# A stacked attention kernel: L1's weight preparation placed among the first batch's top-k, and the last batch's gathered sums shared between GpSimd and DVE

## The chip, the cores and the metric

The kernel runs on one core of a Trainium2 chip. The metric is the device time of one execution in microseconds (us); smaller is better. The core has a matrix engine (TensorE, "PE" in the profile, its weight loads "PEld"), a vector engine (VectorE, "DVE"), an activation engine (ScalarE, "ACT"), GpSimd ("POOL"), and SyncE ("SP"), whose queue issues the DMA transfers. Each engine executes its own instructions strictly in order; between engines there are semaphores.

## The reference, cut to what matters

Four layers are applied to x (32 batches, 128 channels, 1024 positions) with a context ctx of the same shape.

```python
x = L0(x, ctx, ctx, ctx, mask, ...)   # attention within chunks of 64 positions, 8 heads, then layer norm
x = L1(x, ctx, Wq, Aq, Bq, ...)       # 32 query heads, 8 key/value heads; every weight is W + 2 * A @ B (A, B of rank 16)
x = L2(x, ctx, ctx, ctx, mask, ...)   # as L0 with other weights
x = L3(ctx, x, ...)                   # points: see below

def L3(x_loc, x, ...):                # the first 3 channels of ctx are 3-D points
    idx = top_k(-squared_distances(x_loc), 30)          # for each of 1024 points, per batch
    rel = pts[idx] - pts                                 # gathered coordinates
    sph = (rho, theta, phi)(rel)
    h   = three small batch-normalised layers over ALL batches (sph)
    att = softmax(h over the 30 neighbours)
    return x + sum_k x[idx_k] * att_k
```

(The top-k runs over all 128 context channels, as the reference writes it: the distance is the product of whole ctx columns.) The batch norm in L3 needs all batches' gathered coordinates before anything after it can start. So the kernel has two halves: the loop over 32 batches (L0, L1, L2, the top-k and the gathering of coordinates), and after it the batch norms and the weighted sums.

## The kernel before, in words

**The loop over batches.** For batch b, `layers(b)` is a generator that emits L0, L1 and L2 in small pieces, mostly matmuls on PE, row maxima and normalisation on DVE (`mx`, `rc`, `on`) and exponentials on ACT (`s`). Beside it runs `neighbours(b)`, a generator of 64 steps: eight tiles of 128 points, for each four rounds of "find the 8 largest" on DVE. A step is either `V.max` (profile: MAX8) or `V.max_index` with `V.match_replace` (FIND_INDEX8, MATCH_REPLACE8). The same steps emit the distances of the next tile (`distances`: PE matmuls `pd`, an ACT copy to `v`), the norms of the next batch's points (`norms`: `sq`, `xx_ps`, `xp`, `xe`), the gather of the batch before (`gather`) and the angles of a finished pair of batches (`sph`).

**What sets the order.** `InOrder` keeps the instructions of DVE, ACT, PE and GpSimd in the order in which the Python code emits them. The main loop hands out the steps: each piece of `layers(b)` yields a weight, the weights of a batch sum to 65.3 (`STEPS`), and after each piece so many steps of `neighbours(b)` are emitted that their number keeps up with the sum (`done * STEPS < at * LN`). DMA issues on SP are not held in this order; a scheduler places them, and SP executes them in order.

**L1's weights.** Before the loop, at lines 452 to 465, the products 2·A·B are added to the four weights. They are cut into 10 slices of 128 partitions x 8 x 256 (4 for q, 1 for k, 1 for v, 4 for o). For each slice: one load of 1 MB into `w` (pool `wst`, 3 buffers), 8 matmuls of 16 x 128 by 16 x 256 into `lora_ps` (pool `mm_ps`, 2 buffers), 8 DVE instructions that add the product to `w`, and one store of 1 MB to DRAM (`w1_d`). Every batch loads the slices from there again (`w1_slice`). Only when all this is emitted come `norms(0)` and `distances(0, 0, h)` and then the loop.

**The gather.** `gather()` walks over n = 0 to 511: batch, tile of 128 points, half of the 30 neighbours. For one n: a DMA broadcasts rows of indices into `oh` (`spread`, 3 buffers, issued two n ahead), DVE compares them with the partition number to make one-hot matrices (`compare`, one n ahead), PE multiplies them with a table in three groups of 5 (`gps`, one buffer), ACT copies each group into `sel` (2 buffers), and GpSimd sums `sel` in six instructions: two adds of 128x360, one multiply by the mask `el`, adds of 128x180 and 128x90, and one of 128x45 into `co`. The gather of batch b is emitted in the steps of batch b + 1. The 16 n of the last batch are therefore emitted after the last `layers`, in `neighbours(B, coordinates)` and the loop behind it (lines 942 to 945), where the angles of batches 28 and 29 (`sph(14)`) are emitted between them; then comes `sph(15)` for the last two batches, and then the batch norms.

Of the kernel before, what the change touches and what calls it, by code (L numbers as in the profile page):

```python
# [10 lines left out]
F32 = mybir.dt.float32  # L11
# [4 lines left out]
ALU = mybir.AluOpType  # L16
# [4 lines left out]
P = 128  # L21
B, C, T = 32, 128, 1024
# [9 lines left out]
KV = NKV * HD  # L32
R = 16
# [23 lines left out]
def bcast(ap, axis, n):  # L57

    v = ap.unsqueeze(axis)
    shape = list(v.shape)  # L60
    shape[axis] = n
    return v.to_broadcast(shape)
# [3 lines left out]
def stacked_xattn_kernel(ctx: ExitStack, tc: tile.TileContext, io: dict, out: bass.AP):  # L66
    nc = tc.nc
    V, S, PE, G = nc.vector, nc.scalar, nc.tensor, nc.gpsimd
# [42 lines left out]
    NKB, SW = T // P, 256  # L111
# [12 lines left out]
    act = sa.enter_context(tc.tile_pool(name="act", bufs=7))  # L124
# [129 lines left out]
    lofs, cos, els, ohs = {}, {}, {}, {}  # L254
    H = KN // 2

    def spread(n):

        oh = kw.tile([P, H, P], BF16, name="oh", bufs=3)
        b, t, h = n // (2 * NT), n // 2 % NT, n % 2  # L260
        nc.sync.dma_start(
            oh.rearrange("p k n -> p (k n)"),
            hi_d[b * NT + t, h * H : (h + 1) * H, :].rearrange("k n -> (k n)").partition_broadcast(P),
        )
        ohs[n] = oh

    def compare(n):


        b, t, h = n // (2 * NT), n // 2 % NT, n % 2  # L270
        V.tensor_scalar(ohs[n], ohs[n], iota_p, None, ALU.is_equal)
        if h == 0:
            els[b, t] = kw.tile([P, NT, KN], BF16, name="el")
            V.tensor_tensor(els[b, t], iota_l, bcast(lofs[b][:, t, 0:KN], 1, NT), ALU.is_equal)

    def gather():

        last = 2 * NT * B
        for n in range(last):
            b, t, h = n // (2 * NT), n // 2 % NT, n % 2  # L280
            if n == 0:
                spread(0)
                spread(1)
                yield
                compare(0)
                yield
            if b % 2 == 0 and t == 0 and h == 0:
                cos[b // 2] = kw.tile([P, 3, CW], F32, name="co")
            co = cos[b // 2]
            oh = ohs.pop(n)  # L290
            sel = kw.tile([P, H, 9, NT], F32, name="sel")
            for k0 in range(0, H, 5):
                gps = g_ps.tile([P, 5, 9 * NT], F32, name="gps", tag="g")
                for k in range(5):
                    PE.matmul(
                        gps[:, k, :],
                        oh[:, k0 + k, :],
                        ctab[:, b].rearrange("p i e l -> p (i e l)"),
                        start=True,
                        stop=True,  # L300
                    )
                S.copy(sel[:, k0 : k0 + 5].rearrange("p k i l -> p k (i l)"), gps)
                if k0 == 0 and n + 2 < last:
                    spread(n + 2)
                if k0 == H // 3 and n + 1 < last:
                    compare(n + 1)
                if k0 == 2 * H // 3:

                    a = sel.rearrange("p k (i e) l -> p (k i) e l", e=3)
                    a0 = a[:, :, 0, :]  # L310
                    G.tensor_tensor(a0, a0, a[:, :, 1, :], ALU.add)
                    G.tensor_tensor(a0, a0, a[:, :, 2, :], ALU.add)
                    a3 = a0.rearrange("p (k i) l -> p k i l", i=3)
                    ks = slice(h * H, (h + 1) * H)
                    G.tensor_tensor(a3, a3, bcast(els[b, t][:, :, ks].rearrange("p l k -> p k l"), 2, 3), ALU.mult)
                    G.tensor_tensor(a0[:, :, 0:4], a0[:, :, 0:4], a0[:, :, 4:8], ALU.add)
                    G.tensor_tensor(a0[:, :, 0:2], a0[:, :, 0:2], a0[:, :, 2:4], ALU.add)
                    c0 = ((b % 2) * NT + t) * KN + h * H
                    G.tensor_tensor(
                        co[:, :, c0 : c0 + H].rearrange("p i k -> p k i"), a3[:, :, :, 0], a3[:, :, :, 1], ALU.add  # L320
                    )
                yield
# [126 lines left out]

    for nm, n in (("q", T), ("k", KV), ("v", KV), ("o", T)):
        at = act.tile([R, T], F32, name=f"at_{nm}", tag="a4")
        nc.sync.dma_start(at, io[f"A{nm}T"])
        bt = act.tile([R, n], F32, name=f"bt_{nm}", tag="a4")
        nc.sync.dma_start(bt, io[f"B{nm}"])
        for j in range(n // SW):
            c0 = j * SW
            w = wst.tile([P, NKB, SW], F32, name="w1")
            nc.sync.dma_start(w, io[f"W{nm}"].rearrange("(k p) n -> p k n", p=P)[:, :, c0 : c0 + SW])  # L460
            for kb in range(NKB):
                ps = mm_ps.tile([P, SW], F32, name="lora_ps", tag="mm")
                PE.matmul(ps, at[:, kb * P : kb * P + P], bt[:, c0 : c0 + SW], start=True, stop=True)
                V.scalar_tensor_tensor(w[:, kb, :], ps, LORA, w[:, kb, :], ALU.mult, ALU.add)
            nc.sync.dma_start(w1_d[nm][j], w.rearrange("p k n -> p (k n)"))

    def w1_slice(nm, j):
        w = wst.tile([P, NKB, SW], F32, name="w1")
        nc.sync.dma_start(w.rearrange("p k n -> p (k n)"), w1_d[nm][j])
        return w  # L470
# [447 lines left out]
    V, S, PE, G = (InOrder(tc, e) for e in (nc.vector, nc.scalar, nc.tensor, nc.gpsimd))  # L918
    for _ in norms(0):
        pass  # L920
    for h in range(2):
        distances(0, 0, h)
    coordinates = gather()
    LN = NT * TK
    STEPS = 65.3
    for b in range(B):
        near = neighbours(b, coordinates)
        done, at = 0, 0.0
        for w in layers(b):
            if w > 0.0:  # L930
                for a in tails:
                    next(a, None)
            at += abs(w)
            while done < LN and done * STEPS < at * LN:
                next(near, None)
                done += 1
        assert abs(at - STEPS) < 1e-6, at
        for _ in near:
            pass
# [9 lines left out]
    V, S, PE, G = nc.vector, nc.scalar, nc.tensor, nc.gpsimd  # L949
# [9 lines left out]
    with ExitStack() as st:  # L959
# [37 lines left out]
        def bn_coefs(name, mu, var, n, g, bb):  # L997

            a = l3.tile([P, n], F32, name=f"a_{name}")
            cst = l3.tile([P, n], F32, name=f"c_{name}")  # L1000
            S.activation(a, var, AF.Sqrt, bias=eps_t)
            V.reciprocal(a, a)
            V.tensor_tensor(a, a, g, ALU.mult)
            V.tensor_tensor(cst, mu, a, ALU.mult)
            V.tensor_tensor(cst, bb, cst, ALU.subtract)
            return a, cst
# [46 lines left out]
        for c in range(NCK):  # L1053
            x = [co[:, c, i, :] for i in range(3)]
            y = []
            for j in range(6):
                z = work(f"z{j}")
                if j < NZ:
                    ps = z_ps.tile([P, CW], F32, name="z_ps")
# [8 lines left out]
            for i in range(3):  # L1068
                if i < NH:
                    ps = h_ps.tile([P, CW], F32, name="h_ps")  # L1070
# [14 lines left out]
        for c in range(NCK):  # L1085
# [4 lines left out]
            ps = h_ps.tile([P, CW], F32, name="h_ps")  # L1090
# [4 lines left out]
        a3, c3 = bn_coefs("3", *moments("3", st3, 1), 1, g3, b3)  # L1095
# [55 lines left out]
    steps, done = deque(), []  # L1151
# [36 lines left out]
    def load(b):  # L1188

        x3t = ab.tile([P, NT, C], F32, name="x3t", bufs=3)  # L1190
        nc.sync.dma_start(x3t, x3_d[:, b * NT * C : (b + 1) * NT * C])
        at = ab.tile([P, NT * KR], F32, name="att")
        nc.sync.dma_start(at, att_d[:, b * NT * KR : (b + 1) * NT * KR])
        h1 = ab.tile([P, 2 * NT * NG], BF16, name="h1")
        nc.sync.dma_start(h1, hl_d[:, b].rearrange("p e n -> p (e n)"))
        hl = ab.tile([P, 2, NT, NG, 2], BF16, name="hl")
        S.copy(hl.rearrange("p e t g c -> p (e t g) c"), bcast(h1, 2, 2))
        att = ab.tile([P, NT * KR], F32, name="attt")
        V.transpose(att, at)
        ap = ab.tile([P, 2, NT, NG, 2], F16, name="ap")  # L1200
        a0, a1 = (ap[:, i].rearrange("p t g c -> p (t g) c") for i in range(2))
        S.activation(a0, bcast(att, 2, 2), AF.Copy, scale=AS)
        V.scalar_tensor_tensor(a1, bcast(att, 2, 2), AS, a0, ALU.mult, ALU.subtract)
        xs = ab.tile([P, 2, NT, C], F16, name="xs", bufs=3)
        S.activation(xs[:, 0], x3t, AF.Copy, scale=XS)
        V.scalar_tensor_tensor(xs[:, 1], x3t, XS, xs[:, 0], ALU.mult, ALU.subtract)
        return x3t, xs, hl, ap
# [21 lines left out]
    for b in range(B):  # L1229
        x3t, xs, hl, ap = ready  # L1230
        for T4 in range(NT // 4):
# [3 lines left out]
            for t4 in range(4):  # L1235
                t = 4 * T4 + t4
# [13 lines left out]
                for h in range(2):  # L1250

                    ps = at_ps.tile([P, NG // 2, 4, 2, NT], F32, name="at_ps")
# [71 lines left out]
```

## Time and profile before

| | us |
|---|---|
| three runs, median (lowest to highest) | 7793.85 (7787.23 to 7795.2) |
| the profiled execution, its own time | 7792.81 |
| its span from first to last instruction | 7791.0 |
| PE, DVE, ACT, POOL busy in it | 6478.1, 6707.4, 4266.8, 2870.5 |
| granted TensorE clock, mean | 0.895 |

The page cuts the span into 40 slices of 195 us and prints one digit for each: the share of a slice in which an engine was busy, in tenths. The timeline prints one line per instruction, or per run of equal ones: start, duration, engine, source line, operation, output<-inputs, the count, and in brackets how long the engine had been idle and what ended that. Everything inside the main loop has line L54, because it goes through the helper of `InOrder`; it is told apart by the tiles' names. The profiled execution is 1.04 us faster than the median of the runs shown.

### The profile page before, as it was taken

The numbers are of one execution on the slowest core, as the hardware profiler recorded it, in microseconds if no ns is written. First come the engines' busy times: TensorE is split into PE (matmuls) and PEld (weight loads), VectorE is DVE, ScalarE is ACT, GpSimd is POOL, SyncE is SP. The second block draws the span as 40 slices with busy tenths as digits, with TensorE's granted clock in tenths as the row PEclk, the third lists the DMA queues.
The fourth block names the chain that finished last, engine by engine and source line by source line (L and its number), as shares of the span: only waits on it lengthen the run. The fifth ranks groups of instructions, "written<-read, shape, count | busy, mean of one in ns | idle before, by whom it ended". The sixth has DMA issues, their size and how long they took to land.

```text
span 7791.0 us, 152295 instructions
## 1 busy us (share of the span) xinstructions
PE 6478.1 (83%) x60911; PEld 4501.3 (58%) x61331; DVE 6707.4 (86%) x9607; ACT 4266.8 (55%) x10867; POOL 2870.5 (37%) x3788
## 2 busy tenths in 40 slices
PE   6888888888888888888888888888888882958998
PEld 3666565656565666566666666666656561435555
DVE  4888888888888888888989888888888886989998
ACT  1555555555555555555555555555555552357787
POOL 0144444444444434444444444444444446000000
PEclk9999898989898989898888888888889895979999
DMA  5333332333333323333333333333333223013332
GB/s 148 103 127 125 103 114 98 117 102 114 102 114 107 115 91 115 107 115 108 114 105 114 110 114 107 112 107 114 110 105 110 98 101 113 0 55 97 97 93 74
DMA packets 327717, 813.28 MB, mean 104 GB/s; under 512 B 95712, under 2 KB 184320, under 8 KB 284768
## 3 DMA queue, kind: packets, MB, share of 16 engines
q1 hardware_dynamic: 327008, 803.53, 31.3%
q8 instruction: 482, 7.90, 0.4%
q14 instruction: 227, 1.86, 0.1%
HBM read 703.54 MB, written 66.32 MB: 99 GB/s over the span
## 4 chain that ended last, share of the span: by engine, by line
PE 46%; DVE 30%; ACT 14%; POOL 4%; issue 3%; DMA 2%; SPq 0%; another core or an unknown queue 0%; DVEq 0%; ACTq 0%; POOLq 0%
PE tr L54 9%; PE s_ps L54 7%; PE o_ps L54 7%; DVE idx L54 5%; PE q_ps L54 5%; DVE top L54 5%; PE pd L54 4%; DVE v L54 4%; ACT s L54 4%; POOL sel L54 3%; PE gps L54 2%; DVE oh L1241 2%; PE h_ps L1042 2%; PE k_ps L54 2%; DVE mx L54 2%
## 5 line engine op out<-in xcount | busy, mean ns | idle before, releaser
L54 POOL TENSOR_TENSOR sel<-sel 128x360 f32<-128x360 f32 (+2 forms) x2048 | 1550.8, 757 | 2867.5 <-ACT sel L54 2747.1
L54 DVE MAX8 top<-v 128x8 f32<-128x1024 f32 x1024 | 1248.5, 1219 | 91.4 <-ACT v L54 81.4
L54 ACT ACTIVATE s<-s_ps,mx 128x64 f32<-128x64 f32 (+1 forms) x5120 | 1194.0, 349 | 118.0 <-DVE mx L54 117.6
L54 DVE FIND_INDEX8 idx<-top,v 128x8 uint32<-128x1024 f32 x1024 | 1246.9, 1218 | 0.0
L54 ACT COPY sel<-gps 128x360 f32<-128x360 f32 x1536 | 714.2, 465 | 946.4 <-PE gps L54 892.4
L54 ACT COPY pt<-tr 128x512 f32<-128x512 f32 x768 | 450.8, 587 | 895.9 <-PE tr L54 894.6
L54 DVE MATCH_REPLACE8 v<-top,v 128x1024 f32<-128x1024 f32 x768 | 928.5, 1209 | 0.0
L54 PEld LDWEIGHTS <-oh 128*128 128x128 bf16 x7680 | 483.6, 107 | 501.7 <-issue 429.8
L54 PE MATMUL gps<-ctab,oh 128*128 128x72 bf16 x7680 | 549.9, 208 | 265.7 <-ACT sel L54 262.4
L54 DVE TENSOR_REDUCE mx<-s_ps 128x8 f32<-128x512 f32 (+1 forms) x768 | 524.0, 682 | 283.6 <-PE s_ps L54 283.4
L54 PE MATMUL tr<-ident,s 128*128 128x128 f32 x3072 | 575.2, 310 | 183.8 <-ACT s L54 177.3
L1162 PE MATMUL po<-wt,xs 128*128 128x512 f16 x2048 | 692.5, 383 | 0.0
L54 PEld LDWEIGHTS tr<-ident,s 128*128 128x128 f32 x3072 | 447.1, 158 | 422.9 <-ACT s L54 237.5
L1258 PE MATMUL at_ps<-wz,oh 128*128 128x64 f16 x8192 | 572.3, 194 | 137.8 <-ACT wt L1263 65.8
L1258 PEld LDWEIGHTS <-oh 128*128 128x128 f16 x8192 | 442.3, 99 | 396.6 <-issue 181.0
L54 PE MATMUL pd<-cx 128*128 128x512 f32 x1024 | 640.7, 711 | 0.8 <-ACT v L54 0.8
L54 POOL TENSOR_TENSOR sel<-sel,el 128x360 f32<-128x360 f32 x512 | 615.3, 1202 | 40.2
L54 PE MATMUL tr<-half 128*128 128x512 bf16 x1536 | 522.7, 426 | 113.3 <-ACT ot L54 68.3
L1263 ACT CAST wt<-at_ps 128x512 f16<-128x512 f32 x1024 | 544.0, 595 | 121.3 <-PE at_ps L1258 120.6
L1241 DVE TENSOR_TENSOR oh<-iot,hl 128x8192 f16<-128x8192 bf16 x128 | 565.6, 4419 | 4.3 <-PE at_ps L1258 2.7
L54 ACT ACTIVATE v<-pd,nxx 128x512 f32<-128x512 f32 x512 | 358.8, 701 | 319.6 <-PE gps L54 133.8
L54 PE MATMUL q_ps<-xt,w 128*128 128x128 f32 x4096 | 507.4, 279 | 1.7
(232 smaller groups left out, 11851.4 us busy)
## 6 DMA issues: line engine op xcount, KB each, us to landing
oh<-hi_d SPq DMA_DIRECT2D x512, 480.0 KB
w<-w_q SPq DMA_DIRECT2D x128, 1024.0 KB
w<-w_o SPq DMA_DIRECT2D x128, 1024.0 KB
w<-w_k SPq DMA_DIRECT2D x32, 1024.0 KB
w<-w_v SPq DMA_DIRECT2D x32, 1024.0 KB
wz<-wp SPq DMA_DIRECT2D x256, 128.0 KB
cx<-in_ctx SPq DMA_DIRECT2D x32, 512.0 KB
xin<-in_x SPq DMA_DIRECT2D x32, 512.0 KB
```

The source lines that it names most:

```text
L54: return lambda *a, **k: self.tc.keep_in_program_order(f(*a, **k))
L1042: PE.matmul(ps, d[:, i, :], x[i], start=(i == 0), stop=(i == len(x) - 1))
L1162: PE.matmul(po[0], xs[:, i, l, :], wt[:, j, l, :, :].rearrange("p t n -> p (t n)"), start=(n == 0), stop=(n == 4 * NT - 1),)
L1241: V.tensor_tensor(pairs(oh2), pairs(bcast(iot, 1, 2 * NG)), by_twos(h2, P // 2), ALU.is_equal)
L1258: PE.matmul(ps[:, g], oh[:, gg], wz_now[:, :, t4 * NG + gg], start=True, stop=True)
L1263: S.copy(wt[:, i, :, t4, :].rearrange("p l (q g) -> p l q g", g=NG)[:, :, :, h * (NG // 2) : (h + 1) * (NG // 2)], ps[:, :, :, i, :].rearr ...
```

## The change

Two places are edited.

1. The preparation of L1's weights becomes a generator `prepared()` that yields after each of the 10 slices, with the loads of two slices issued ahead. It is emitted in the main loop at b = 0, before `layers(0)`; after each slice, 5 steps of `neighbours(0)` are emitted. So 50 of the 64 top-k steps of batch 0 stand between the slices and 14 are left for `layers(0)`; `norms(0)` and the first distances now come before the preparation. Its PE and DVE instructions go through `InOrder` now, so their line becomes L54.
2. For the last batch, the six summing instructions of odd n are issued on DVE instead of GpSimd. They stand in DVE's order where they stood in the code: behind `compare(n + 1)` and, in `neighbours(B)`, behind a step of the angles.

```diff
                 if k0 == 2 * H // 3:
+                    E = V if b == B - 1 and n % 2 else G
                     a = sel.rearrange("p k (i e) l -> p (k i) e l", e=3)
                     a0 = a[:, :, 0, :]
-                    G.tensor_tensor(a0, a0, a[:, :, 1, :], ALU.add)
-                    G.tensor_tensor(a0, a0, a[:, :, 2, :], ALU.add)
+                    E.tensor_tensor(a0, a0, a[:, :, 1, :], ALU.add)
+                    E.tensor_tensor(a0, a0, a[:, :, 2, :], ALU.add)
...

-    for nm, n in (("q", T), ("k", KV), ("v", KV), ("o", T)):
-        at = act.tile([R, T], F32, name=f"at_{nm}", tag="a4")
-        nc.sync.dma_start(at, io[f"A{nm}T"])
-        bt = act.tile([R, n], F32, name=f"bt_{nm}", tag="a4")
-        nc.sync.dma_start(bt, io[f"B{nm}"])
-        for j in range(n // SW):
-            c0 = j * SW
+    def prepared():
+        def load(nm, j):
             w = wst.tile([P, NKB, SW], F32, name="w1")
-            nc.sync.dma_start(w, io[f"W{nm}"].rearrange("(k p) n -> p k n", p=P)[:, :, c0 : c0 + SW])
+            nc.sync.dma_start(w, io[f"W{nm}"].rearrange("(k p) n -> p k n", p=P)[:, :, j * SW : j * SW + SW])
+            return w
+
+        slices = [(nm, n, j) for nm, n in (("q", T), ("k", KV), ("v", KV), ("o", T)) for j in range(n // SW)]
+        ws = [load(nm, j) for nm, n, j in slices[:2]]
+        for i, (nm, n, j) in enumerate(slices):
+            if j == 0:
+                at = act.tile([R, T], F32, name=f"at_{nm}", tag="a4")
+                nc.sync.dma_start(at, io[f"A{nm}T"])
+                bt = act.tile([R, n], F32, name=f"bt_{nm}", tag="a4")
+                nc.sync.dma_start(bt, io[f"B{nm}"])
+            w = ws.pop(0)
             for kb in range(NKB):
                 ps = mm_ps.tile([P, SW], F32, name="lora_ps", tag="mm")
-                PE.matmul(ps, at[:, kb * P : kb * P + P], bt[:, c0 : c0 + SW], start=True, stop=True)
+                PE.matmul(ps, at[:, kb * P : kb * P + P], bt[:, j * SW : j * SW + SW], start=True, stop=True)
                 V.scalar_tensor_tensor(w[:, kb, :], ps, LORA, w[:, kb, :], ALU.mult, ALU.add)
             nc.sync.dma_start(w1_d[nm][j], w.rearrange("p k n -> p (k n)"))
+            if i + 2 < len(slices):
+                ws.append(load(slices[i + 2][0], slices[i + 2][2]))
+            yield
...
         near = neighbours(b, coordinates)
         done, at = 0, 0.0
+        if b == 0:
+            for _ in prepared():
+                for _ in range(5):
+                    next(near, None)
+                    done += 1
         for w in layers(b):
```

More of the change, by code (lines that the diff above doesn't have):

```diff
@@ L307, in gather @@
                 if k0 == 2 * H // 3:
+                    E = V if b == B - 1 and n % 2 else G
                     a = sel.rearrange("p k (i e) l -> p (k i) e l", e=3)
                     a0 = a[:, :, 0, :]
-                    G.tensor_tensor(a0, a0, a[:, :, 1, :], ALU.add)
-                    G.tensor_tensor(a0, a0, a[:, :, 2, :], ALU.add)
+                    E.tensor_tensor(a0, a0, a[:, :, 1, :], ALU.add)
+                    E.tensor_tensor(a0, a0, a[:, :, 2, :], ALU.add)
                     a3 = a0.rearrange("p (k i) l -> p k i l", i=3)
                     ks = slice(h * H, (h + 1) * H)
-                    G.tensor_tensor(a3, a3, bcast(els[b, t][:, :, ks].rearrange("p l k -> p k l"), 2, 3), ALU.mult)
-                    G.tensor_tensor(a0[:, :, 0:4], a0[:, :, 0:4], a0[:, :, 4:8], ALU.add)
-                    G.tensor_tensor(a0[:, :, 0:2], a0[:, :, 0:2], a0[:, :, 2:4], ALU.add)
+                    E.tensor_tensor(a3, a3, bcast(els[b, t][:, :, ks].rearrange("p l k -> p k l"), 2, 3), ALU.mult)
+                    E.tensor_tensor(a0[:, :, 0:4], a0[:, :, 0:4], a0[:, :, 4:8], ALU.add)
+                    E.tensor_tensor(a0[:, :, 0:2], a0[:, :, 0:2], a0[:, :, 2:4], ALU.add)
                     c0 = ((b % 2) * NT + t) * KN + h * H
-                    G.tensor_tensor(
+                    E.tensor_tensor(
                         co[:, :, c0 : c0 + H].rearrange("p i k -> p k i"), a3[:, :, :, 0], a3[:, :, :, 1], ALU.add
```

## The prediction

> **What bounds the kernel now.** I read the 40 slices first, to see which stages the edit touches and which engine is full there.
>
> ```profile
> PE   6888888888888888888888888888888882958998
> DVE  4888888888888888888989888888888886989998
> POOL 0144444444444434444444444444444446000000
> ```
>
> Only the two ends of the loop matter: slice 1, where DVE is at 4, and slices 33 and 34, where PE falls to 2. (In the middle PE and DVE are both at 8, and nothing is edited.) Next the timeline of DVE from 68 to 152 us shows how the preparation ends and batch 0 begins:
>
> ```profile
> 68.92 0.76 DVE L464 SCALAR_TENSOR_TENSOR w<-lora_ps,w 128x256 f32<-128x256 f32 x2 [8.09 <-DMA w<-in_Wq]
> 70.65 0.42 DVE L464 SCALAR_TENSOR_TENSOR w<-lora_ps,w 128x256 f32<-128x256 f32 x1 [0.98 <-PE lora_ps L463]
> 71.50 0.42 DVE L464 SCALAR_TENSOR_TENSOR w<-lora_ps,w 128x256 f32<-128x256 f32 x1 [0.43 <-PE lora_ps L463]
> ...
> 144.04 1.23 DVE L54 MAX8 top<-v 128x8 f32<-128x1024 f32 x1 [12.01 <-ACT v L54]
> 145.31 0.09 DVE L54 MATCH_VALUE_LOAD idx<-top,v 128x8 f32 x1
> 145.38 1.22 DVE L54 FIND_INDEX8 idx<-top,v 128x8 uint32<-128x1024 f32 x1
> 146.64 0.09 DVE L54 MATCH_VALUE_LOAD v<-top,v 128x8 f32 x1
> 146.72 1.21 DVE L54 MATCH_REPLACE8 v<-top,v 128x1024 f32<-128x1024 f32 x1
> 147.96 1.23 DVE L54 MAX8 top<-v 128x8 f32<-128x1024 f32 x1
> ...
> 151.76 0.68 DVE L54 TENSOR_REDUCE mx<-s_ps 128x8 f32<-128x512 f32 x1
> ```
>
> In the preparation one DVE addition takes 0.42 us and then waits 0.43 to 0.46 us for the next product: 0.87 us each. So DVE has gaps, but gaps of 0.4 us, in which no top-k instruction of 1.2 us fits. Top-k starts at 144.04, the first row maximum of L0 at 151.76.
>
> Third, busy time by stretch, for the preparation, batch 0 from its first row maximum to the start of batch 1 (306 us), and the last batch's sums:
>
> ```profile
> core 0: us, PE busy (x) PEld busy (x) DVE busy (x) ACT busy (x) POOL busy (x), PEclk, DMA share, GB/s
> 37.00:132.00 95.00, 71.47 (x163) 40.85 (x162) 33.60 (x80) 2.34 (x2) 0.00 (x0) 1.00 0.67 234
> 152.00:306.00 154.00, 137.11 (x1222) 99.27 (x1232) 131.96 (x208) 77.19 (x232) 8.16 (x13) 0.94 0.22 74
> 6459.00:6546.00 87.00, 20.16 (x220) 14.97 (x219) 35.81 (x43) 22.92 (x48) 79.59 (x101) 0.50 0.24 77
> ```
>
> Batch 0 has two full engines: PE 137 of 154 us, DVE 132. The last sums have one: POOL, 80 of 87. Their timeline shows the cycle of one n:
>
> ```profile
> 6512.00 2.45 POOL L54 TENSOR_TENSOR sel<-sel 128x360 f32<-128x360 f32 x2
> 6512.08 0.46 ACT L54 COPY sel<-gps 128x360 f32<-128x360 f32 x1 [2.42 <-POOL co L54]
> 6513.08 0.46 ACT L54 COPY sel<-gps 128x360 f32<-128x360 f32 x1 [0.55 <-PE gps L54]
> 6514.09 0.46 ACT L54 COPY sel<-gps 128x360 f32<-128x360 f32 x1 [0.54 <-PE gps L54]
> 6514.52 1.11 POOL L54 TENSOR_TENSOR sel<-sel,el 128x360 f32<-128x360 f32 x1
> ```
>
> ACT starts filling a `sel` when POOL has finished the n two before; the three copies take 2.5 us, hidden behind POOL's sum of the n between.
>
> **Part 1, the preparation.** Removed: the stretch before 144 us in which nothing but slices runs. Added in front of L0: 50 top-k steps. Both are serial on DVE, so I walk along DVE.
>
> Start. On SP batch 0's `cx` load moves ahead of all slices, to where `at_q` is issued now (31.94 us). Landing: between 2.3 us (bt_q, 64 KB, issued 34.44, used 36.71) and 5.7 us (this load at 104.03, landed at 109.73, among stores); I take 5, near the 5.3 us of the first 1 MB slice, so 37. Then table load 1.28 and square 1.06 on ACT, `xx_ps` 3.57 on PE, and from there to the end of the second `pd` 7.79 (135.07 to 142.86): 50.7. PE's first `lora_ps` is behind that; its product reaches DVE about 1.3 us later (a buffer freed at 42.64, the addition that uses it at 43.95), at 52.0. Eight additions, 7 x 0.87 + 0.42, end at 58.5. The other 9 slices have two products waiting, as after the stall at 68.92: first addition to the end of the eighth (75.39) is 6.5 us, 58.5 in all. DMA is not late: a slice is needed every 15 us and its load and store take about 5 each; the later `at`/`bt` loads and the stores wait on SP behind one another, but all have a block of top-k ahead of their use.
>
> Steps. Two steps take 3.92 us (144.04 to 147.96); a tile's last round lacks the replacement, 2.6. A tile is 3 x 3.92 + 2.6 = 14.4; 50 steps are six tiles and two steps, 90.1 us. `pd` (PE) and `v` (ACT) run beside them, as do `norms(1)` on ACT, PE and POOL, and are not late: a tile's last `v` is due three steps (5 us) after its `pd` is emitted.
>
> So the first row maximum comes at 58.5 + 58.5 + 90.1 = 207.1 instead of 151.8: **+55.3 us**. The matmuls of L0's start are ready by then.
>
> Given back in batch 0. DVE loses about 88 us of top-k there, but PE does not: of the 15 `pd` sets in 152 to 306 us (16.9 us of PE) 11 move out, 12.4 us, and `xx_ps`, 3.4 us. PE's idle time is 16.9 us; the waits of PE show 5.0 as one gap (`tr` for the layer norm's output, late because top-k stands between its DVE instructions), and the rest as 0.7 us waits for ACT copies that stay. I take 5 of the gap and 2 more: 12.4 + 3.4 + 7 = **22.8 us**. Bounds: 15.8 (no idle time returns) to 32.7 (all of it does). PE is late next.
>
> The Trainium skill ("Perfetto Trace Analysis", Identifying the Most-Contended Engine) speaks against my reading: matmul busy time is a bad measure, weight-load busy time a better one. By its measure batch 0 has 55 us of slack on PE, and the sum below would be about -17; that is my second rival.
>
> **Part 2, the sums.** Eight of the last 16 sums leave POOL. The trace has no such sum on DVE. Its 480-element add takes 0.65 us undisturbed (6554.46) and its six-element one 0.17, so 360, 180, 90 and 45 elements are near 0.53, 0.35, 0.26 and 0.21: 3 x 0.53 + 0.82 + starts = 2.7 us. Beside POOL it is slower: from 6491.6 to 6497.4 DVE needed 5.8 us for instructions that take 3.46 alone (four of 0.66, two of 0.41), and POOL 5.86 for a sum of 4.6. So 2.7 (alone) to 4.5 (x 1.67) on DVE, 4.6 to 5.9 on POOL; I take about 3.6 and 5.2, since half of DVE's sum falls into POOL's wait.
>
> That wait is new. POOL's next even n needs the `sel` of the even n just finished: the 2.5 us of copies are no longer hidden. A pair is 2.5 + 5.2 + 0.1 = 7.8 us against 9.6 now (nine sums from 6502.4 to 6545.8: 4.82 each).
> While `sph(14)` runs (n = 497 to 503), DVE is the late one: two compares and `el` 1.9, an angle step near 6.3 (octants, 5.4 to 7.9 beside POOL), then the odd sum behind it, with compare(n + 1) and so PE and ACT waiting behind that. Such a pair is 11 to 12 us against 10.8 (seven sums in 37.8 us). One is only arctangents on ACT: shorter. Walking it: sums 497, 499, 501, 503 end at 6467, 6476, 6488, 6499.5; POOL starts 504 at 6499.3 (today 6507.1, with 503 done before it at 6502.4), then every 7.8 us: 510 ends at 6527.8, DVE's 511 at 6529. The subtraction `r` of `sph(15)`, today at 6545.86, starts 17 us earlier: **-17 us**. Behind it nothing changes. Bounds: -22 (DVE's sum wholly hidden, POOL 4.6: pairs of 7.2) to 0 (sums on the two engines never overlap: 4.6 + 2.7 + 2.5 = 9.8 a pair).
>
> The lower bound is what the Trainium skill ("SBUF — State Buffer", SBUF: two separate sides) says: a DVE instruction with two SBUF inputs and a GpSimd one lock the shared port for a whole instruction each. The row above disagrees: 3.46 + 4.6 us of work in 5.86. By the rule the sum would be +32.
>
> **Sum.** 55.3 - 22.8 - 17 = +15.5 us on the profiled execution's 7792.81; it lies 1 us under the median, so I put the change on 7793.85: **7809 us**, 0.2% slower. That is about what a measurement of this kernel can tell from no change (0.2%, 15.6 us), so the sign of the sum is firmer than the verdict.
>
> **Rivals.**
> 1. Batch 0 gives back all of PE's idle time, 32.7 us, or the slices run at the clock to which `q_ps` warms between 143.08 and 150.72 us (1.91 to 1.02 us for two matmuls; some 1.5 us a slice). +5.6 or about 0: 7794 to 7800, no change. For it: many small waits vanish with the top-k. Against: `lora_ps` stayed slow through 21 us of unbroken work.
> 2. Faster: PE is not really full in batch 0, its ends being modelled. With weight loads busy 99 of 154 us, up to 55 us come back: 55.3 - 55 - 17 = -17, 7777. It turns negative when batch 0 returns 38 us and reads as faster at 54. Against: the 1222 matmuls leave gaps of under 0.7 us, and the batches with a gather on top take longer.
> 3. The tail gains nothing (no overlap, or DVE's angles delay the odd sums more): +32, 7826. For it: the slowed rows above; in the first half DVE has more to do than POOL.
> That the top-k hides nothing at all is half of the forecast: DVE pays for both in turn.
>
> **Chances and range.** Forecast 0.51 (its range, +2 to +30, straddles the limit: 0.27 slower, 0.24 same), rival 1 0.15 (0.13 same, 0.01 each side), rival 2 0.12 (faster), rival 3 0.22 (slower). So slower 0.50, same 0.37, faster 0.13. The range leaves out most of rival 2 and the worst of rival 3: 7782 to 7829.
>
> **What would show it.** First row maximum of L0 near 207 us; additions in runs of eight over 6.5 us between top-k blocks of 9 us; batch 0 from there to batch 1's start about 131 us with PE over 90% busy; at the end POOL idle 2.5 us before each even sum, odd sums of 2.7 to 4.5 us on DVE, and from the end of batch 31 to `r` 17 us less than now. Wrong would make it: batch 0 in under 116 us, slices much under 6.5 us, or sums that do not overlap.

## The result, and the profile after

Over 19 runs of each kernel the change takes 7814.5 us (median; 7794.44 to 7829.16), the kernel before 7789.79 (7775.65 to 7795.2): a ratio of 1.0032, with a 95% interval of 1.0025 to 1.0039. It is slower, by about 25 us (20 to 30 by the interval); 15.5 were forecast, and 7814.5 lies in the range given.

The profiled execution took 7808.19 us, 15.4 more than that of before. That this is nearly the forecast is chance, as the sum by stages shows. From the timelines I read the starts of a few landmarks: DVE's first top-k instruction, the first row maximum of L0, ACT's first `q` of batch 1, the transpose of batch 31's indices that ends its top-k, and the subtraction `r` of `sph(15)`. The stretches between them, in us:

| | first top-k | first row maximum | batch 1 starts | batch 0 | loop to batch 31's indices | from there to `r` | `r` to the end |
|---|---|---|---|---|---|---|---|
| before | 144.0 | 151.8 | 306.0 | 154.2 | 6121.6 | 118.3 | 1245.1 |
| after | 56.2 | 201.6 | 337.3 | 135.7 | 6113.4 | 109.3 | 1246.4 |
| after minus before | | +49.8 | +31.3 | -18.5 | -8.2 | -9.0 | +1.3 |

The edit stands in the start, batch 0 and the stretch to `r`: 49.8 - 18.5 - 9.0 = **+22.3 us**, against +24.7 between the medians. One profile does not fix batch 0 that well: in three experiments below that leave the start as it was, batch 1 starts at 308.6 to 312.1 us and not at 306.0; by them the sum would be +16 to +20. The loop in between is not edited; it took 6121.6 and 6113.4 us in these two executions (mean granted clock 0.895 and 0.896) and 6012.8 to 6106.8 in those of the experiments below (0.899 to 0.911), with the same code. Whole times therefore move by more than most of the effects looked for here: a ratio stands only between runs measured together, and the stretches of the edited stages are the finer reading.

The 40 slices after, for the three engines shown before:

```profile
PE   5888888888888888888888888888888882958998
DVE  6588888888888888888988888888888898989998
POOL 0044444444444444444444444444444445000000
```

DVE rose from 4 to 6 in slice 1, and fell to 5 in slice 2, which holds batch 0 without its top-k: the top-k has been moved, not hidden. At the end, in slice 34, POOL goes from 6 to 5 and DVE from 6 to 8. DVE's timeline at the first block:

```profile
55.82 0.42 DVE L54 SCALAR_TENSOR_TENSOR w<-lora_ps,w 128x256 f32<-128x256 f32 x1 [0.43 <-PE lora_ps L54]
56.16 1.22 DVE L54 MAX8 top<-v 128x8 f32<-128x1024 f32 x1
...
63.98 1.23 DVE L54 MAX8 top<-v 128x8 f32<-128x1024 f32 x1
65.13 0.74 DVE L54 SCALAR_TENSOR_TENSOR w<-lora_ps,w 128x256 f32<-128x256 f32 x2
66.84 0.42 DVE L54 SCALAR_TENSOR_TENSOR w<-lora_ps,w 128x256 f32<-128x256 f32 x1 [0.98 <-PE lora_ps L54]
67.69 0.42 DVE L54 SCALAR_TENSOR_TENSOR w<-lora_ps,w 128x256 f32<-128x256 f32 x1 [0.43 <-PE lora_ps L54]
...
71.16 0.42 DVE L54 SCALAR_TENSOR_TENSOR w<-lora_ps,w 128x256 f32<-128x256 f32 x1 [0.43 <-PE lora_ps L54]
71.50 0.08 DVE L54 MATCH_VALUE_LOAD idx<-top,v 128x8 f32 x1
```

Each block of five steps runs 9 us without a gap; behind it two products wait ("x2"), and from the third on PE is late again by 0.43 to 0.98 us for every addition. A slice costs 6.4 us (65.13 to 71.50), though two of its products were made under the top-k.

Busy time in two stretches, batch 0 (first row maximum to batch 1) and batch 31's indices to `r`; of the kernel before:

```profile
152.00:306.00 154.00, 137.11 (x1222) 99.27 (x1232) 131.96 (x208) 77.19 (x232) 8.16 (x13) 0.94 0.22 74
6427.50:6545.80 118.30, 29.61 (x286) 20.85 (x285) 51.33 (x69) 29.83 (x61) 98.40 (x123) 0.51 0.25 79
```

And of the kernel after (columns: length, then PE, PEld, DVE, ACT and POOL busy with their instructions, PE's clock, DMA share, GB/s):

```profile
201.60:337.30 135.70, 121.01 (x1181) 89.02 (x1182) 55.83 (x106) 68.18 (x217) 5.26 (x7) 0.97 0.25 84
6450.70:6560.00 109.30, 29.74 (x286) 20.62 (x285) 80.34 (x117) 29.83 (x61) 64.71 (x76) 0.51 0.28 86
```

In batch 0 DVE lost 76 us of work. The batch is 18.3 us shorter, of which 16.1 is time that PE is no longer busy (the `pd` and `xx_ps` that moved out are 16.0 of it); PE's idle time only falls from 16.9 to 14.7. In the last sums POOL has 34 us less to do and DVE 29 more, for 9 us.

### The profile page after: what moved, and what is told of

Read it like the earlier page. It is cut to its first block, busy times and chain, and to the rows that moved or that the text cites. A ratio compares the mean times of both kernels' runs of the same rounds, so it can differ in the third digit from the quotient of the medians.

```text
span 7806.4 us, 152322 instructions
## 1 busy us (share of the span) xinstructions
PE 6494.1 (83%) x60918; PEld 4502.2 (58%) x61331; DVE 6740.3 (86%) x9655; ACT 4267.1 (55%) x10867; POOL 2835.7 (36%) x3740
## 3 DMA queue, kind: packets, MB, share of 16 engines
q1 hardware_dynamic: 327008, 803.53, 31.3%
## 4 chain that ended last, share of the span: by engine, by line
PE 46%; DVE 31%; ACT 14%; issue 3%; POOL 3%; DMA 2%; SPq 0%; another core or an unknown queue 0%; ACTq 0%; DVEq 0%; POOLq 0%
PE tr L54 9%; PE s_ps L54 7%; PE o_ps L54 7%; DVE idx L54 6%; DVE top L54 5%; PE q_ps L54 5%; DVE v L54 4%; PE pd L54 4%; ACT s L54 4%; PE gps L54 2%; DVE oh L1259 2%; PE h_ps L1060 2%; PE k_ps L54 2%; POOL sel L54 2%; DVE oh L54 2%
## 5 line engine op out<-in xcount | busy, mean ns | idle before, releaser
L54 POOL TENSOR_TENSOR sel<-sel 128x360 f32<-128x360 f32 x2016 | 1525.9, 757 | 2878.2 <-ACT sel L54 2759.6
L54 DVE MAX8 top<-v 128x8 f32<-128x1024 f32 x1024 | 1248.0, 1219 | 67.8 <-ACT v L54 57.5
L54 ACT ACTIVATE s<-s_ps,mx 128x64 f32<-128x64 f32 (+1 forms) x5120 | 1194.1, 349 | 116.3 <-DVE mx L54 116.0
L54 DVE FIND_INDEX8 idx<-top,v 128x8 uint32<-128x1024 f32 x1024 | 1246.4, 1217 | 0.0
L54 ACT COPY sel<-gps 128x360 f32<-128x360 f32 x1536 | 714.1, 465 | 940.8 <-PE gps L54 907.2
L54 ACT COPY pt<-tr 128x512 f32<-128x512 f32 x768 | 450.8, 587 | 896.5 <-PE tr L54 890.7
L54 DVE MATCH_REPLACE8 v<-top,v 128x1024 f32<-128x1024 f32 x768 | 928.4, 1209 | 0.0
L54 DVE TENSOR_REDUCE mx<-s_ps 128x8 f32<-128x512 f32 (+1 forms) x768 | 522.9, 682 | 311.6 <-PE s_ps L54 306.7
L54 PEld LDWEIGHTS <-oh 128*128 128x128 bf16 x7680 | 483.8, 107 | 495.8 <-issue 402.1
L54 PE MATMUL gps<-ctab,oh 128*128 128x72 bf16 x7680 | 550.4, 208 | 259.9 <-ACT sel L54 236.3
L54 PE MATMUL tr<-ident,s 128*128 128x128 f32 x3072 | 575.6, 310 | 184.1 <-ACT s L54 177.3
L54 PEld LDWEIGHTS tr<-ident,s 128*128 128x128 f32 x3072 | 447.2, 158 | 422.5 <-ACT s L54 237.5
L1276 PE MATMUL at_ps<-wz,oh 128*128 128x64 f16 x8192 | 573.8, 194 | 137.9 <-ACT wt L1281 66.4
L54 PE MATMUL pd<-cx 128*128 128x512 f32 x1024 | 655.9, 726 | 1.7 <-ACT v L54 1.7
L54 POOL TENSOR_TENSOR sel<-sel,el 128x360 f32<-128x360 f32 x504 | 608.7, 1208 | 39.5
L54 PE MATMUL tr<-half 128*128 128x512 bf16 x1536 | 522.0, 425 | 110.5 <-ACT ot L54 66.5
L54 ACT ACTIVATE v<-pd,nxx 128x512 f32<-128x512 f32 x512 | 358.7, 701 | 428.1 <-remote 146.1
L54 PE MATMUL q_ps<-xt,w 128*128 128x128 f32 x4096 | 505.1, 278 | 1.6
```

The lines of the kernel that those rows point to most:

```text
L54: return lambda *a, **k: self.tc.keep_in_program_order(f(*a, **k))
L1276: PE.matmul(ps[:, g], oh[:, gg], wz_now[:, :, t4 * NG + gg], start=True, stop=True)
```

## Experiments

**Each part alone.** The first kernel has the new preparation and all sums on GpSimd, the second the old preparation and the sums by turns.

```diff
 # part 1 alone
-                    E = V if b == B - 1 and n % 2 else G
+                    E = G
```

> Part 1 alone: the preparation among the top-k, all sums on GpSimd. Theory (the two parts add up; the loss is all in part 1): first row maximum of L0 at 201.6 us and batch 1 at 337 as in the changed kernel, so +31 us there, and the stretch from the last batch's index transpose to r at 118 us as before; the whole +31 us, 0.4%. Rival (the parts are not independent, or the main loop in between pays for some of it): less than +25 or more than +37 with these two stretches unchanged.

> Part 2 alone: the last batch's odd sums on DVE, the preparation as before. Theory: the start is as before (row maximum at 151.8, batch 1 at 306), the stretch from the last index transpose to r falls from 118.3 to 109.3 us, the whole -9 us. My prediction had -17; rival (the changed kernel's tail was disturbed by what came before it): 101 us for the stretch.

Part 1 alone: first row maximum at 201.7, batch 1 at 335.8 (306.0 before: +29.8), 117.9 us to `r`. The time is 7792.8 us, a ratio of 1.0039 (1.0026 to 1.0053): 0.39% of the 7763.72 us that the kernel before took beside it is 30 us (20 to 41), the same as the stage shows. Part 2 alone: a start as before (151.9) and 109.2 us to `r`, 9 less; a ratio of 0.9995 (0.9986 to 1.0004), in which 9 us (0.12%) still fits. In its profile batch 0 took 160.2 us instead of 154.2 with no edit there; two more kernels below that leave the start as it was have 155.8 and 157.5. PE's idle time in the four is 16.6 to 18.1 us; the rest is PE's busy time, 137.1 to 142.1 us at granted clocks of 0.91 to 0.95. So about 6 us of this stretch are not settled by one profile. In the other stretches each part does alone what it does in the changed kernel, and the loss is part 1's.

**How much top-k between the slices.** Part 1 alone with 2 steps and with none after each slice:

```diff
-                for _ in range(5):
+                for _ in range(2):      # and range(0)
```

> Part 1 without the top-k steps: loads two slices ahead and the norms first, but 0 steps between the slices; all 64 steps stay in batch 0. Theory (the loss is the 50 steps, 1.76 us each, that DVE pays in turn with the slices): slices of 7.0 us from 49.8 us on, end near 120, row maximum near 128 instead of 151.8, batch 0 as long as before (154 us), the whole -24 us. Rival (the loss is in the slices, their loads or the new place of the norms): row maximum at 152 or later, no gain or a loss.

> Part 1 with 2 steps between the slices instead of 5, so 20 steps moved. Theory: 20 x 1.76 = 35 us more of preparation than with none, less 5 us because two products wait at each slice; row maximum near 153; batch 0 gives back about 0.38 us a step, 7 us; the whole about -5 us, between the kernels with 0 and with 5 steps and on the line through them. Rival (a few steps are hidden in the gaps of the preparation and only the later ones cost): as fast as with 0 steps, -24 us.

| steps after a slice | first row maximum | batch 0 | batch 1 starts | whole time, ratio |
|---|---|---|---|---|
| (before) | 151.8 | 154.2 | 306.0 | |
| 0 | 137.9 | 157.9 | 295.8 | 0.9990 (0.9981 to 0.9999) |
| 2 | 154.6 | 149.9 | 304.5 | 0.9993 (0.9984 to 1.0002) |
| 5 | 201.7 | 134.1 | 335.8 | 1.0039 (1.0026 to 1.0053) |

Part 1 holds a gain, the loads issued ahead, and a loss, the top-k; the last 30 steps cost 31.3 us at batch 1, 1.04 us a step. The first 20 cost only 8.7, 0.43 a step. At the first row maximum, which does not carry the unsettled us of batch 0, it is 16.7 us for the first 20 and 47.1 for the last 30: 0.84 and 1.57 a step. The first steps are cheaper because without steps the slices have a wait that the steps then cover. DVE's first row maximum without steps came 10 us later than I had expected (128), the whole gained about 8 us and not 24, and the timelines of that run say why. PE's:

```profile
90.42 0.63 PE L54 MATMUL lora_ps<-bt_v,at_v 16*128 16x256 f32 x1
101.25 3.35 PE L54 MATMUL lora_ps<-bt_o,at_o 16*128 16x256 f32 x7 [10.21 <-DMA bt_o<-in_Bo]
```

And that of SP's queue:

```profile
91.53 0.32 SPq L474 DMA_DIRECT2D w_v<-w  x1
91.91 0.43 SPq L458 DMA_DIRECT2D w<-in_Wo  x1
92.43 1.10 SPq L466 DMA_DIRECT2D at_o<-in_AoT  x1
93.58 0.82 SPq L468 DMA_DIRECT2D bt_o<-in_Bo  x1
```

The two factors of `o`, 64 KB each, are issued on SP only behind the store of the slice before (which waits for its last addition) and behind a load of 1 MB. They are asked for at 92.4 us, when PE already needs them, and are there at 101.2. With 2 steps after a slice PE has no such wait, and in the changed kernel DVE never waits for a load; a block of top-k covers this.

**Does batch 0's top-k hold PE up?** The kernel before, without DVE's work for the first 50 steps; the layers, distances and loads stay.

```diff
             for r in range(KR // 8):
-                V.max(top, v)
+                skip = b == 0 and 8 * t + 2 * r < 50
+                if not skip:
+                    V.max(top, v)
...                                   # likewise max_index and match_replace
```

> The kernel before, but the DVE instructions of the first 50 top-k steps of batch 0 are left out (about 88 us of DVE); the distances on PE and their copies on ACT stay. Theory (batch 0 is bound by PE): row maximum near 150, batch 0 shorter by about 4 us, the whole -5 us. Rival (DVE's top-k holds batch 0 up, and the give-back of the changed kernel was small for another reason): batch 0 shorter by 20 us or more.

Batch 0 took 145.6 us, 8.6 less than in the profile of before, between theory and rival:

```profile
149.00:294.70 145.70, 133.11 (x1241) 95.09 (x1239) 55.86 (x105) 77.33 (x232) 8.14 (x13) 1.00 0.22 78
```

PE is busy for 133 of the 145.7 us: 4.0 us less busy time, at a granted clock of 1.00 instead of 0.94, and 4.3 less idle time. So the waits for top-k were worth 4 to 5 us (PE's idle time is 16.6 to 18.1 us in the four batches without an edit, 12.6 here), and 50 steps, about 88 us of DVE, were nearly free where they stood. One thing stays open: in every profile with all the top-k in batch 0 its clock is 0.91 to 0.95, and in the three with at most 14 steps left there it is 0.97 to 1.00. Whether the top-k itself costs PE some us by the clock, no run tells apart from drift. The ratio, 0.9952 (0.989 to 1.0015), has too wide an interval to add to that (the kernel before took 7671 to 7783 us in this series); the same holds for the next two kernels (1.0056, 0.9994 to 1.0119, and 0.9951, 0.9886 to 1.0015), which are read by their stages.

**What bounds the sums by turns.** Part 2 alone with a third `sel`, and with all sixteen sums on DVE.

```diff
 # third buffer
-            sel = kw.tile([P, H, 9, NT], F32, name="sel")
+            sel = kw.tile([P, H, 9, NT], F32, name="sel", bufs=3)
 # all sums on DVE
-                    E = V if b == B - 1 and n % 2 else G
+                    E = V if b == B - 1 else G
```

> Part 2 alone with three sel buffers instead of two. Theory (the odd chain bounds the tail: odd sum, then the compare two ahead behind it on DVE, then matmuls and copies of that n, then its sum): only the waits in which the copy of an odd n had been given the buffer of the even n before it go (5 us and 1.5 us), the stretch from the last index transpose to r falls from 109 to about 103 us. Rival (my prediction: GpSimd's wait for the copies of its next n bounds the pairs): the wait goes, pairs of 5.3 us instead of 8.7, the stretch falls to 95 us or less.

> All 16 sums of the last batch on DVE, none on GpSimd: nothing to contend with. Theory (beside GpSimd a DVE sum takes up to 6.9 us, alone 2.9): every sum 2.9 us, every compare 0.72, the stretch from the last index transpose to r about 108 us, as with the sums shared. Rival (the two engines do not disturb each other, the sums are slow in themselves): sums of 4 us and more, the stretch over 120 us.

The third buffer gives 107.7 us to `r`, 1.6 less than two: the copies behind POOL were not the bound. In the changed kernel the timelines of POOL, PE and DVE show the loop that was. The last adds of `sph(14)` on POOL (`r`), and POOL's even sums behind them (first two adds of each):

```profile
6522.49 4.55 POOL L54 TENSOR_TENSOR r<-co 128x480 f32<-128x480 f32 x3 [4.71 <-DVE co L54]
6527.00 2.07 POOL L54 TENSOR_TENSOR sel<-sel 128x360 f32<-128x360 f32 x2
6536.16 2.39 POOL L54 TENSOR_TENSOR sel<-sel 128x360 f32<-128x360 f32 x2 [3.58 <-ACT sel L54]
6544.14 2.05 POOL L54 TENSOR_TENSOR sel<-sel 128x360 f32<-128x360 f32 x2 [2.64 <-ACT sel L54]
6553.04 2.15 POOL L54 TENSOR_TENSOR sel<-sel 128x360 f32<-128x360 f32 x2 [3.59 <-ACT sel L54]
```

PE's first product of a pair:

```profile
6529.89 0.48 PE L54 MATMUL gps<-ctab,oh 128*128 128x72 bf16 x5 [7.09 <-DVE oh L54]
...
6537.80 0.48 PE L54 MATMUL gps<-ctab,oh 128*128 128x72 bf16 x5 [2.28 <-DVE oh L54]
...
6546.77 0.48 PE L54 MATMUL gps<-ctab,oh 128*128 128x72 bf16 x5 [3.26 <-DVE oh L54]
```

DVE, an odd sum with POOL beside it, the next one in a wait of POOL, and the compares behind each:

```profile
6522.33 1.97 DVE L54 TENSOR_TENSOR sel<-sel 128x360 f32<-128x360 f32 x2
6524.34 1.64 DVE L54 TENSOR_TENSOR sel<-sel,el 128x360 f32<-128x360 f32 x1
6526.01 2.17 DVE L54 TENSOR_TENSOR sel<-sel 128x180 f32<-128x180 f32 x2
6528.22 0.99 DVE L54 TENSOR_TENSOR co<-sel 128x45 f32<-128x45 f32 x1
6529.12 2.20 DVE L54 TENSOR_SCALAR oh<-oh,iota_p 128x1920 bf16<-128x1920 bf16 x2
...
6533.53 1.07 DVE L54 TENSOR_TENSOR sel<-sel 128x360 f32<-128x360 f32 x2
6534.64 0.78 DVE L54 TENSOR_TENSOR sel<-sel,el 128x360 f32<-128x360 f32 x1
6535.45 0.65 DVE L54 TENSOR_TENSOR sel<-sel 128x180 f32<-128x180 f32 x2
6536.14 0.27 DVE L54 TENSOR_TENSOR co<-sel 128x45 f32<-128x45 f32 x1
6536.33 2.74 DVE L54 TENSOR_SCALAR oh<-oh,iota_p 128x1920 bf16<-128x1920 bf16 x2
```

POOL starts a sum every 8.7 us (6527.00 to 6553.04 is three pairs), not every 7.8, and with the third buffer still every 8.7 (6490.03 to 6515.99 in that run). PE's first product waits for the compare, `oh`, which stands on DVE behind the odd sum; three groups of products and copies, 3.0 us, lead to the next odd sum, and behind that stands the next compare. In this loop the four odd sums took 2.9, 3.5, 2.9 and 3.3 us. The two compares behind a sum took 2.2 to 3.0 us (one alone 0.71), and DVE's other work, the mask `el` and the batch norm statistics of the angles, held two of the odd sums up by another 0.6 and 0.9. Only two odd sums were much longer, 5.1 us and the 6.9 of the first one shown; both stand before this loop, while `sph(14)` runs. With three buffers ACT's first copy of a pair waits for the same thing, the product behind the compare:

```profile
6493.43 0.46 ACT L54 COPY sel<-gps 128x360 f32<-128x360 f32 x1 [7.96 <-PE gps L54]
```

With all sums on DVE the stretch is 106.6 us, shorter than by turns, though one engine now does what two did. DVE's timeline of that run, one n of it without any other work, and an earlier sum:

```profile
6393.85 1.97 DVE L54 TENSOR_TENSOR sel<-sel 128x360 f32<-128x360 f32 x2
6395.85 1.64 DVE L54 TENSOR_TENSOR sel<-sel,el 128x360 f32<-128x360 f32 x1
6397.52 1.53 DVE L54 TENSOR_TENSOR sel<-sel 128x180 f32<-128x180 f32 x2
6399.09 0.27 DVE L54 TENSOR_TENSOR co<-sel 128x45 f32<-128x45 f32 x1
...
6421.01 1.09 DVE L54 TENSOR_TENSOR sel<-sel 128x360 f32<-128x360 f32 x2
6422.13 0.77 DVE L54 TENSOR_TENSOR sel<-sel,el 128x360 f32<-128x360 f32 x1
6422.94 0.65 DVE L54 TENSOR_TENSOR sel<-sel 128x180 f32<-128x180 f32 x2
6423.62 0.27 DVE L54 TENSOR_TENSOR co<-sel 128x45 f32<-128x45 f32 x1
6423.81 0.71 DVE L54 TENSOR_SCALAR oh<-oh,iota_p 128x1920 bf16<-128x1920 bf16 x1
6424.44 1.09 DVE L54 TENSOR_TENSOR sel<-sel 128x360 f32<-128x360 f32 x2
```

From one sum to the next it is 3.43 us (6421.01 to 6424.44), 6.9 a pair against 8.7 by turns and 9.6 on GpSimd. The first sum shown took 5.5 us instead of 2.9: it runs beside the one thing that POOL still does there, the last three adds of `sph(14)`:

```profile
6394.01 4.54 POOL L54 TENSOR_TENSOR r<-co 128x480 f32<-128x480 f32 x3 [38.10 <-DVE co L54]
```

The same three adds took 3.50 us for `sph(15)` in the kernel before (at 6573.93), with no sum on DVE beside them. So 2.8 us of DVE and 3.5 of POOL, 6.3 apart, took 5.5 together: the two gained 0.8 us from running at once. The Trainium skill ("SBUF — State Buffer", SBUF: two separate sides) calls the port that the two engines share an exclusive lock for a whole instruction, for a DVE instruction with two SBUF inputs beside a GpSimd one that reads SBUF. These sums come near to it; the row weighed in the prediction, 3.46 and 4.6 us of work in 5.86, does not.

**Do the gains add up?** First the start without steps beside a third `sel`; then, after the wait for `bt_o` had been found, the two factors of a matrix loaded with its first slice, two slices ahead; and that start with all sums on DVE.

```diff
 # without steps, factors loaded ahead
             if i + 2 < len(slices):
+                if slices[i + 2][2] == 0:
+                    factors(slices[i + 2][0], slices[i + 2][1])    # at, bt
                 ws.append(load(slices[i + 2][0], slices[i + 2][2]))
...
-                for _ in range(5):
+                for _ in range(0):
```

> The changed kernel with 0 steps between the slices and three sel buffers. Theory: the gains of the two add up, row maximum near 128, stretch to r about 103 us, the whole -39 us against the kernel before. Rival (the main loop takes it back): less than half of that.

> Part 1 with no top-k step between the slices, part 2 undone, and the two lora factors of a matrix loaded together with its first slice, two slices ahead, instead of at their use. In the run without steps but with the old place of these loads PE waited 10.2 us, from 91 to 101 us, for bt_o, which stood on SP behind two stores. Theory: that wait was all that the slices had of stalls beside two of 1 us; with it gone the first top-k is at 120 us (130.2 there, 144.0 before), the first row maximum of L0 at 128 and batch 1 at 286 (306.0 before). Rival: the DMA queue itself is late (its share is near 1 there), and the wait only moves to a slice: first top-k at 127 to 130. Tail as before, 118.

> The same start, and all sixteen sums of the last batch on DVE. Theory: the gains stand in different stages and add up: first top-k at 120 us, batch 1 at 286, and 106.6 us from the last index transpose to the subtraction r of sph(15) (118.3 before); in all 20 + 12 = 32 us less than the kernel before, 0.4%. Rival: batch 0, started earlier, is met by a later weight slice or by the throttle and gives the start back: 12 us less, 0.15%.

| | first top-k | first row maximum | batch 0 | batch 1 starts | to `r` | ratio |
|---|---|---|---|---|---|---|
| no steps, third `sel` | 131.4 | 139.1 | 158.6 | 297.7 | 107.1 | 0.9994 (0.9934 to 1.0055) |
| no steps, factors ahead | 120.5 | 129.4 | 160.1 | 289.6 | 117.8 | 0.9960 (0.9947 to 0.9974) |
| the same, all sums on DVE | 120.3 | 129.4 | 159.5 | 288.8 | 106.2 | 0.9938 (0.9925 to 0.9951) |

In the first the stages gain as each did alone; its whole time can't be told from that of before. In the second the wait of 10 us is gone, as the theory had it: in DVE's timeline three waits of about 1 us for slices are left, where the kernel before had three of about 8 (8.09 at 68.92, 7.88 at 97.14, 8.07 at 125.55).

```profile
71.38 0.76 DVE L54 SCALAR_TENSOR_TENSOR w<-lora_ps,w 128x256 f32<-128x256 f32 x2 [0.98 <-DMA w<-in_Wq]
...
92.83 0.76 DVE L54 SCALAR_TENSOR_TENSOR w<-lora_ps,w 128x256 f32<-128x256 f32 x2 [1.11 <-DMA w<-in_Wo]
...
107.15 0.82 DVE L54 SCALAR_TENSOR_TENSOR w<-lora_ps,w 128x256 f32<-128x256 f32 x2 [0.91 <-DMA w<-in_Wo]
```

Batch 0 then takes 5 to 6 us longer than in the profile of before: rows show PE busier (141.9 of 159.4 us at a clock of 0.93, against 137.1 of 154.0 at 0.94). Batch 0 without an edit took up to 160.2, so this need not come from the edit.

The third, at 7641.62 us against 7691.96 for the kernel before measured beside it, is faster than both kernels of this case. By stages it saves 17.2 at batch 1 and 12.1 before `r`, 29 us, or 32 to 35 against the other starts of batch 1 without an edit (308.6 to 312.1); the ratio says 38 to 58. What is left of that, no stretch of an edited stage shows.

## Why the prediction was right, and where it was off

The sum and its sign held: +22.3 us by stages and about +25 in the runs, against +15.5. Part of that is luck: the start was 5.5 us better than forecast, batch 0 and the sums 4.3 and 8 worse, and the three errors partly cancel. Its argument, that DVE pays for both the slices and the top-k in turn while batch 0 gives back only what PE had to do, is what the runs show. By its terms:

- **The start: +49.8 us instead of +55.3.** The first addition came at 49.77 us (52.0 predicted), so 2.2 us of the 5.5 are `norms(0)` and the first `pd`, which were ready earlier. The rest, 3.3 us, is in the walk: nine slices of 6.4 us instead of 6.5, and 88 us for the 50 steps instead of 90.1.
- **Given back in batch 0: 18.5 us instead of 22.8.** The moved work of PE was right (15.8 predicted, 16.1 less busy time measured). The 7 us of idle time was not: only 2.2 came back (2 to 4, if part 1 alone and the other batches without an edit are taken in). The 4.3 us by themselves would prove nothing, as batch 0 without an edit varies by 6. The gap of 5.0 us before `tr` that I put down to top-k between DVE's instructions shrank only to 2.2, and it is 2.2 with those 50 steps left out too, so less than 3 of it were top-k's. The waits of PE in batch 0 (columns: total, times, longest) of the kernel before:

```profile
PE tr L54 <- ACT xt L54: 5.0, 1, 5.0
```

And of the kernel after:

```profile
PE tr L54 <- ACT xt L54: 2.9, 2, 2.2
```

- **PE was full, as read.** The second rival, PE with 55 us of slack because its weight loads were busy for only 99 of 154 us, fell: with 76 us less on DVE, batch 0 gave back 2.2 us beyond the work that PE lost. The Trainium skill ("Perfetto Trace Analysis", Identifying the Most-Contended Engine) would have PE's headroom judged by weight-load busy time, beside a share of peak FLOP/s that I did not work out; in this stage matmul busy time, 137 of 154 us, told better what could come back.
- **The first rival, all idle time given back, fell too**: 14.7 us of it were still there after.
- **The sums: -9 us instead of -17.** This is the term that was mis-sized most, by 8 us. It fell short in both halves of the tail. From POOL's sum of n = 504 to `r` it gained 5.8 us and not 9.2. There the sums themselves were sized well: 5.2 to 5.6 us on POOL (5.2 taken) and 2.9 to 3.5 on DVE (3.6 taken). The path was wrong: the step "a pair is 2.5 + 5.2 + 0.1 = 7.8 us" took the copies behind POOL's own buffer for the bound, but POOL waited 2.6 to 3.6 us for the loop through DVE (odd sum, compare, products and copies), and a pair took 8.7. The third buffer, which left that at 8.7, showed it. Before n = 504, while `sph(14)` runs, 3.3 us were gained and not 7.8: two odd sums took 5.1 and 6.9 us, and two copies waited 5.1 and 6.1 us for a buffer (last section). The third buffer gave back 1.6 us of that; the rest no run takes apart.
- **The third rival was half right**: the tail did gain, but little of that from two engines working at once. Two of the last four odd sums lie wholly in a wait of POOL. DVE alone gains 11.7 us, the two by turns 9.
- **DMA was not late** for DVE in the changed kernel, as said (PE waited 3.3 us for `bt_v`, under a block of top-k). But "all have a block of top-k ahead of their use" was doing work that I did not price: without the blocks `bt_o` cost 10 us.

## What to carry to other kernels

Moving a full engine's work out of a stretch bounded by another engine returns only what the other engine had of it: 50 top-k steps put 64 us in front of batch 0 (201.7 against 137.9 without them) and took 24 out of it (134.1 against 157.9), 21 of them time that PE was busy (119.7 against 140.4; the products that moved are 16 of these). Before an elementwise chain is shared between GpSimd and DVE, try all of it on DVE: 6.9 us a pair alone, 8.7 by turns. And when loads are issued ahead, look on the queue for the small operands that were left at their place of use; two of 64 KB behind a store cost 10 of the 24 us that loading ahead had to give (first top-k at 144.0, then 130.2, then 120.5).

## What the runs showed that I had not expected

- DVE's sum of 2.8 us took 5.5 beside 3.5 us of GpSimd work, which took 4.5 itself: 6.3 us of work in 5.5. The compare on bf16, with one tensor as input, is slowed as well: 2.20 us for two beside POOL, against 0.71 for one alone.
- The two `sel` buffers are not used strictly by turns. In the built program n = 499 has the buffer of 498, and 503 that of 502, so their copies waited for the sum of the n just before, and not two before. ACT's timeline of the changed kernel:

```profile
6495.41 0.46 ACT L54 COPY sel<-gps 128x360 f32<-128x360 f32 x1 [5.14 <-POOL co L54]
...
6517.81 0.46 ACT L54 COPY sel<-gps 128x360 f32<-128x360 f32 x1 [6.14 <-POOL co L54]
```

  I had walked these n as if the buffers alternated. With the third buffer these waits are gone, and 1.6 us with them.
